# Attention scores on two 64-column halves of TensorE's array

## The chip, the cores and the metric

One core of a Trainium2 chip runs the whole program. The metric is device time in microseconds (us), lower is better. Most executions of one kernel agree within 0.3%. Engines: PE is TensorE's matmul, PEld its weight load, DVE VectorE, ACT ScalarE, POOL GpSimd.

## The reference, cut to what matters

```python
# x [128 graphs, 64 tokens, 768], adj [128, 64, 64] of 0 and 1; all fp32
h = relu(layernorm(x))
for l in range(2):
    m_left, m_right = h @ W_left[l].T, h @ W_right[l].T
    u_left  = einsum('bih,bjh->bij', h, m_left)  / sqrt(768)
    u_right = einsum('bih,bjh->bij', h, m_right) / sqrt(768)
    u = u_left * (upper triangle of adj and diagonal) + u_right * (lower triangle of adj)
    e = exp(u) * adj
    attention = e / (e.sum(axis=2) + 1e-10)
    h = relu(layer_norm(attention @ (h @ W_lin[l].T + b_lin[l])))
out = x + h
```

The scores of a graph ("batch" below) are a 64x64 matrix for left and one for right.

## The kernel before

A unit is 512 tokens: Q = 4 pairs of batches (PAIR = 2, S = 64 tokens, P = 128). There are 16 units, and each layer has two passes over them: pass one makes m_left and m_right (`project`), the scores and the attention, and pass two makes h @ W_lin (`linear`), attention times that, and the layer norm. The projections use Strassen's scheme, which is why they come as seven groups X, Y, Z, V, X, Z, V of six matmul instructions each. Instructions are issued in the order of the program; `queue` and `pump` mix small steps in between. An evacuation is the instruction of VectorE or ScalarE that takes a finished result of TensorE out of its result memory (PSUM).

The scores before, once with left and once with right:

```python
def scores(u, k, kind):
    ht, m = HT[1, l, u], M[kind]                 # both [128 features, 6 chunks, 512 tokens]
    p = ps_aux.tile([P, Q, P], F32, name="aux")
    for q in range(Q):
        t = slice(q * P, (q + 1) * P)            # a pair of batches: 128 tokens
        for c in range(C):
            nc.tensor.matmul(p[:, q, :], m[:, c, t], ht[:, c, t],      # stationary, moving
                             start=(c == 0), stop=(c == C - 1))
    ...
    for h in range(PAIR):
        r = slice(h * S, (h + 1) * S)
        nc.vector.tensor_tensor(um[r, k], p[r, :, r], wm[r, :, k, :], op=ALU.mult)
    # then, after the second kind: add, exp, times adj,
    #   a matmul with the block matrix bsum for the sums over j, + eps, reciprocal, product, store
```

`p[r, :, r]` shows that two 64x64 blocks of each 128x128 result are used and two are thrown away. The attention is stored as 64 columns per row, and pass two copies it into zeroed block-diagonal matrices (`expand`, on POOL).

## Time and profile before

| | before |
|---|---|
| median of the first 3 runs | 3460.22 us (3458.72 to 3462.4) |
| PE busy | 3258.6 us, 94% of the span |
| score matmuls, busy time of PE | 353.4 us, 3072 records |
| DVE, POOL, ACT busy | 39%, 26%, 16% |

The lines behind this, and how they are read, are in the prediction.

### The profile page before, as it was taken

How to read it: one execution, taken by the hardware profiler on the slowest of the kernel's cores; microseconds unless marked ns; L12 is line 12 of the kernel's file. 1: busy time of each engine (PE TensorE's matmuls, PEld its weight loads, DVE VectorE, ACT ScalarE, POOL GpSimd, SP SyncE). 2: the span in 40 equal slices, each digit the busy share in tenths (PEclk: the TensorE clock that was granted, in tenths of full speed). 3: DMA queues.
4: the chain of work that ended last, by engine and by line, in shares of the span. 5: the costliest groups of instructions: out<-in, count | busy, mean ns of one | idle time of the engine just before them, and what ended most of it. 6: DMA issues, size and time to landing. Idle time of an engine off the chain costs nothing.

```text
span 3456.8 us, 37506 instructions
## 1 busy us (share of the span) xinstructions
PE 3258.6 (94%) x15168; PEld 2574.7 (74%) x15168; DVE 1347.1 (39%) x2938; ACT 537.1 (16%) x1137; POOL 887.6 (26%) x576
## 2 busy tenths in 40 slices
PE   5999999999999879999989999999999979988987
PEld 4898989898989545555568988989989965544544
DVE  4334333433342324444422322232232226666665
ACT  1111111111111123333310000000000001111111
POOL 3000110011010243223222110010010015766675
PEclk9999999999999989999999999999999989999999
DMA  5111121111110222232221100100010012333332
GB/s 173 48 42 46 42 78 42 46 58 62 46 42 20 96 98 98 76 114 77 76 80 51 45 25 24 42 28 24 30 40 24 23 66 100 130 127 124 139 131 102
DMA packets 77484, 236.25 MB, mean 68 GB/s; under 512 B 7936, under 2 KB 42240, under 8 KB 67072
## 3 DMA queue, kind: packets, MB, share of 16 engines
q1 hardware_dynamic: 77312, 233.86, 18.6%
q8 instruction: 119, 1.95, 0.2%
q14 instruction: 53, 0.43, 0.0%
HBM read 154.15 MB, written 79.69 MB: 68 GB/s over the span
## 4 chain that ended last, share of the span: by engine, by line
PE 82%; POOL 9%; DVE 5%; DMA 2%; ACT 1%; issue 1%; SPq 1%; POOLq 0%; ACTq 0%; DVEq 0%
PE V L235 14%; PE Z L235 14%; PE X L235 14%; PE aux L265 10%; PE Y L235 7%; PE X L455 6%; PE aux L374 5%; POOL z L403 4%; PE Y L455 4%; PE V L455 3%; POOL z L402 3%; PE Z L455 2%; DVE xr L405 2%; PE aux L204 1%; PE aux L421 1%; DVE u L463 1%
## 5 line engine op out<-in xcount | busy, mean ns | idle before, releaser
L120 POOL TENSOR_TENSOR ts<-ht 128x768 f32<-128x768 f32 x64 | 115.7, 1808 | 1592.8 <-DMA ht<-h 781.7
L265 PEld LDWEIGHTS aux<-ht,n 128*128 128x128 f32 x3072 | 352.0, 192 | 2.6
L265 PE MATMUL aux<-ht,n 128*128 128x128 f32 x3072 | 353.4, 275 | 0.0
L455 PE MATMUL X<-w_n_A,ht 128*128 128x384 f32 x768 | 280.5, 503 | 65.5 <-DVE n L472 36.4
L455 PE MATMUL V<-w_n_A,ts 128*128 128x384 f32 x768 | 271.6, 490 | 23.6 <-DVE n L470 23.6
L235 PE MATMUL X<-ht,w_l_A 128*128 128x256 f32 x1152 | 281.7, 381 | 12.3 <-DMA ht<-h 12.3
L235 PE MATMUL X<-ht,w_r_A 128*128 128x256 f32 x1152 | 280.1, 379 | 0.0
L235 PE MATMUL V<-ts,w_r_A 128*128 128x256 f32 x1152 | 280.0, 379 | 0.0
L235 PE MATMUL V<-ts,w_l_A 128*128 128x256 f32 x1152 | 280.0, 379 | 0.0
L455 PEld LDWEIGHTS X<-w_n_A,ht 128*128 128x128 f32 x768 | 144.3, 195 | 172.9 <-DVE n L472 54.9
L235 PEld LDWEIGHTS X<-ht,w_l_A 128*128 128x128 f32 x1152 | 217.4, 191 | 41.1 <-DMA ht<-h 12.7
L235 PEld LDWEIGHTS V<-ts,w_l_A 128*128 128x128 f32 x1152 | 218.8, 190 | 29.7
L235 PEld LDWEIGHTS V<-ts,w_r_A 128*128 128x128 f32 x1152 | 216.8, 190 | 28.3
L455 PEld LDWEIGHTS V<-w_n_A,ts 128*128 128x128 f32 x768 | 141.2, 190 | 128.0 <-issue 22.2
L235 PEld LDWEIGHTS X<-ht,w_r_A 128*128 128x128 f32 x1152 | 215.3, 190 | 27.3
L252 DVE TENSOR_TENSOR n<-Z,u 128x256 f32<-128x256 f32 x192 | 81.5, 425 | 364.6 <-PE Z L235 364.6
L240 ACT COPY s<-X 128x256 f32<-128x256 f32 x192 | 71.4, 372 | 974.9 <-PE X L235 974.9
L243 DVE TENSOR_TENSOR u<-Y,s 128x256 f32<-128x256 f32 x192 | 81.6, 425 | 360.6 <-PE Y L235 357.5
L465 POOL TENSOR_TENSOR u2b<-u,b 128x384 f32<-128x384 f32 x64 | 63.7, 995 | 551.3 <-DVE rs L393 551.2
L250 ACT COPY n<-X 128x256 f32<-128x256 f32 x192 | 71.4, 372 | 778.1 <-PE X L235 778.1
L405 DVE SCALAR_TENSOR_TENSOR xr<-z,xr 128x768 f32<-128x768 f32 x64 | 135.8, 2123 | 130.9 <-POOL z L403 130.9
L272 DVE TENSOR_TENSOR um<-aux,wm 64x256 f32<-64x256 f32 x128 | 54.0, 422 | 325.3 <-PE aux L265 324.5
(100 smaller groups left out, 4798.7 us busy)
## 6 DMA issues: line engine op xcount, KB each, us to landing
ht<-h SPq DMA_DIRECT2D x48, 1536.0 KB, 7.5
x<-in_x_dram SPq DMA_DIRECT2D x64, 384.0 KB, 7.2
h<-ht SPq DMA_DIRECT2D x16, 1536.0 KB, 6.2
h<-n SPq DMA_DIRECT2D x16, 1536.0 KB, 6.1
xr<-in_x_dram SPq DMA_DIRECT2D x64, 384.0 KB, 3.7
out_dram<-xr SPq DMA_DIRECT2D x64, 384.0 KB, 2.5
adj<-in_adj_dram SPq DMA_DIRECT2D x32, 256.0 KB, 3.3
w_l_A<-in_w_left_dram SPq DMA_DIRECT2D x8, 576.0 KB, 10.1
```

What stands on the lines that cost most here:

```text
L120: queue.append(lambda: nc.gpsimd.tensor_sub(b["T1"], b["B12"], b["B11"]))
L235: nc.tensor.matmul(p, w[a][:, c, g * P:(g + 1) * P], b[t][:, c, :], start=(new and c == 0), stop=(c == CH - 1), skip_group_check=True)
L240: nc.scalar.copy(s1, p)
L243: nc.vector.tensor_add(u2, p, s1)
L250: nc.scalar.copy(m[:, g, :TH], p)
L252: nc.vector.tensor_add(m[:, g, TH:], p, u2)
L265: nc.tensor.matmul(p[:, q, :], m[:, c, t], ht[:, c, t], start=(c == 0), stop=(c == C - 1))
L374: nc.tensor.matmul(p[:, :HH], BD[u % 2][:, q, :], hl[:, q, n * HH:(n + 1) * HH], start=True, stop=True)
L402: nc.gpsimd.tensor_mul(z, z, rows["a"])
L403: nc.gpsimd.tensor_add(z, z, rows["b"])
L405: nc.vector.scalar_tensor_tensor(xr, z, 0.0, xr, op0=ALU.max, op1=ALU.add)
L455: nc.tensor.matmul(p, b[t][:, c, r * P:(r + 1) * P], w[a][:, c, :], start=(new and c == 0), stop=(c == CH - 1), skip_group_check=True)
```

## The change

The score matrix is turned: tokens i are rows, so that 64 tokens of one batch are the stationary operand, placed in the left or the right half of the array's columns, and m_left and m_right of that batch lie side by side as 128 moving columns. The sums over j then run along a row, which VectorE can do, and bsum goes. The attention must be transposed for pass two, which TensorE does in pass one, and it is stored as a whole block-diagonal matrix, so the copies of pass two go. Cut to its core:

```diff
-    M[kind] = big.tile([P, C, T], F32, name="n")
+    M[u] = [big.tile([P, CH, T // S, 2, S], F32, name="n") for _ in range(2)]   # left, right side by side
...
-            for q in range(Q):
-                t = slice(q * P, (q + 1) * P)
-                for c in range(C):
-                    nc.tensor.matmul(p[:, q, :], m[:, c, t], ht[:, c, t], ...)
+            for q in range(Q):
+                for c in range(C):
+                    for h in range(PAIR):
+                        b = q * PAIR + h
+                        nc.tensor.matmul(p[h * S:(h + 1) * S, q, :], ht[:, c, b * S:(b + 1) * S],
+                                         m[c // CH][:, c % CH, b].rearrange("p k j -> p (k j)"), ...)
...
-                    nc.tensor.matmul(ps, bsum, v, ...)          # sums over j, then 128x256 reciprocal
+                    nc.vector.reduce_sum(s, v, axis=X)          # [128, 4], reciprocal of that
+                    # v * s into the diagonal blocks of bd, then
+                    for q in range(Q):
+                        nc.tensor.transpose(pt[:, q, :], bd[:, q, :], ident)
...
-    nc.gpsimd.tensor_copy(BD[u % 2][k, :, k], AT[u][k])          # pass two
```

Both kinds are now done in one burst per unit, placed between the second and third matmul group of the next unit.

More of the change, by code (lines that the diff above doesn't have):

```diff
@@ L131 @@
     H1 = [dram.tile([P, C, T], F32, name=f"h1_{u}") for u in range(NB)]
-    ATT = [[dram.tile([P, Q, S], F32, name=f"att{l}_{u}") for u in range(NB)] for l in range(L)]
+    ATT = [[dram.tile([P, Q, P], F32, name=f"att{l}_{u}") for u in range(NB)] for l in range(L)]
     ident = const.tile([P, P], F32, name="ident")
@@ L138 @@
     nc.gpsimd.memset(eps_in, EPS_IN)
-    bsum = const.tile([P, P], F32, name="bsum")
-    nc.gpsimd.memset(bsum, 0.0)
     diff = const.tile([P, S], I32, name="diff")
@@ L146 @@
         r = slice(h * S, (h + 1) * S)
-        nc.gpsimd.memset(bsum[r, r], 1.0)
         nc.gpsimd.iota(diff[r], pattern=[[-1, S]], base=0, channel_multiplier=1)
-    nc.vector.tensor_scalar(tri[:, 0, :], diff, 0.0, None, op0=ALU.is_ge)
-    nc.vector.tensor_scalar(tri[:, 1, :], diff, 0.0, None, op0=ALU.is_lt)
+    nc.vector.tensor_scalar(tri[:, 0, :], diff, 0.0, None, op0=ALU.is_le)
+    nc.vector.tensor_scalar(tri[:, 1, :], diff, 0.0, None, op0=ALU.is_gt)
     BD = []
@@ L183, in masks @@
                 WM[u] = sp.tile([P, Q, 2, S], F32, name="wm")
-                t = tri.rearrange("p k s -> p (k s)").unsqueeze(1).to_broadcast([P, Q, 2 * S])
-                nc.gpsimd.tensor_tensor(WM[u].rearrange("p q k s -> p q (k s)"),
-                                        ADJ[u].rearrange("p q k s -> p q (k s)"), t, op=ALU.mult)
+                for k in range(2):
+                    t = tri[:, k].unsqueeze(1).to_broadcast([P, Q, S])
+                    nc.gpsimd.tensor_tensor(WM[u][:, :, k], ADJ[u][:, :, 1 - k], t, op=ALU.mult)
             def prepare(u):
@@ L221, in pass_one, with project @@
             M = {}
-            def project(u, kind, g):
-                b, w = tokens_of((1, l, u)), W[l, kind]
-                if g == 0:
-                    M[kind] = big.tile([P, C, T], F32, name="n")
-                m = M[kind]
+            def project(u, k, g, between=None):
+                b, w = tokens_of((1, l, u)), W[l, "lr"[k]]
                 bank = {}
@@ L237, in project @@
                                          skip_group_check=True)
+                    if i == 2 and k == 0 and g == 0:
+                        M[u] = [big.tile([P, CH, T // S, 2, S], F32, name="n") for _ in range(2)]
+                    if i >= 3:
+                        half, first = ((1, 4), (0, 0), (0, 4), (1, 0))[i - 3]
+                        to = M[u][half][:, g, first:first + 4, k, :]
+                        pb = p.rearrange("p (b s) -> p b s", s=S)
                     if i == 0:
@@ L246, in project @@
                         nc.vector.tensor_add(u4, p, u2)
-                    elif i == 3:
-                        nc.vector.tensor_add(m[:, CH + g, TH:], p, u4)
                     elif i == 4:
-                        nc.scalar.copy(m[:, g, :TH], p)
-                    elif i == 5:
-                        nc.vector.tensor_add(m[:, g, TH:], p, u2)
-                    else:
-                        nc.vector.tensor_add(m[:, CH + g, :TH], p, u2)
+                        nc.scalar.copy(to, pb)
+                    else:
+                        nc.vector.tensor_add(to, pb, (u4 if i == 3 else u2).rearrange("p (b s) -> p b s", s=S))
@@ L255, in project, with scores @@
+                    if i == 1 and between:
+                        between()
                     pump(1)
-            UM = {}
-            def scores(u, k, kind):
-                ht, m = HT[1, l, u], M[kind]
-                p = ps_aux.tile([P, Q, P], F32, name="aux")
+            def scores(u):
+                ht, m = HT[1, l, u], M[u]
+                p = ps_aux.tile([P, Q, 2 * S], F32, name="aux")
                 for q in range(Q):
-                    t = slice(q * P, (q + 1) * P)
                     for c in range(C):
-                        nc.tensor.matmul(p[:, q, :], m[:, c, t], ht[:, c, t],
-                                         start=(c == 0), stop=(c == C - 1))
-                if k == 0:
-                    UM[u] = sp.tile([P, 2, Q, S], F32, name="um")
-                um, wm, adj = UM[u], WM[u], ADJ[u]
-                for h in range(PAIR):
-                    r = slice(h * S, (h + 1) * S)
-                    nc.vector.tensor_tensor(um[r, k], p[r, :, r], wm[r, :, k, :], op=ALU.mult)
-                if k == 0:
-                    return
+                        for h in range(PAIR):
+                            b = q * PAIR + h
+                            nc.tensor.matmul(p[h * S:(h + 1) * S, q, :], ht[:, c, b * S:(b + 1) * S],
+                                             m[c // CH][:, c % CH, b].rearrange("p k j -> p (k j)"),
+                                             start=(c == 0), stop=(c == C - 1))
+                wm, adj = WM[u], ADJ[u]
@@ L276, in chain @@
                 def chain():
+                    um = sp.tile([P, Q, 2, S], F32, name="um", bufs=1)
+                    nc.vector.tensor_tensor(um.rearrange("p q k j -> p (q k j)"), p.rearrange("p q m -> p (q m)"),
+                                            wm.rearrange("p q k j -> p (q k j)"), op=ALU.mult)
+                    yield
                     v = sp.tile([P, Q, S], F32, name="v", bufs=1)
-                    nc.vector.tensor_add(v, um[:, 0], um[:, 1])
+                    nc.vector.tensor_add(v, um[:, :, 0], um[:, :, 1])
@@ L281, in chain @@
                     yield
-                    nc.vector.tensor_mul(v, v, adj[:, :, 0, :])
+                    nc.vector.tensor_mul(v, v, adj[:, :, 1, :])
+                    s = stat.tile([P, Q], F32, name="s", bufs=2)
+                    nc.vector.reduce_sum(s, v, axis=mybir.AxisListType.X)
                     yield
-                    p2 = ps_aux.tile([P, Q, P], F32, name="aux")
-                    ps = p2.rearrange("p q i -> p (q i)")[:, :Q * S]
-                    nc.tensor.matmul(ps, bsum, v.rearrange("p q i -> p (q i)"), start=True, stop=True)
+                    nc.vector.tensor_scalar_add(s, s, EPS_ATT)
+                    nc.vector.reciprocal(s, s)
+                    bd = BD[u % 2]
+                    for h in range(PAIR):
+                        r = slice(h * S, (h + 1) * S)
+                        nc.vector.tensor_tensor(bd[r, :, r], v[r], s[r].unsqueeze(2).to_broadcast([S, Q, S]),
+                                                op=ALU.mult)
                     yield
-                    s = sp.tile([P, Q, S], F32, name="s", bufs=1)
-                    nc.vector.tensor_scalar_add(s.rearrange("p q i -> p (q i)"), ps, EPS_ATT)
-                    nc.vector.reciprocal(s, s)
                     yield
-                    a = sp.tile([P, Q, S], F32, name="a", bufs=1)
-                    nc.vector.tensor_mul(a, v, s)
-                    nc.sync.dma_start(ATT[l][u], a)
+                    pt = ps_aux.tile([P, Q, P], F32, name="aux")
+                    for q in range(Q):
+                        nc.tensor.transpose(pt[:, q, :], bd[:, q, :], ident)
+                    at = sp.tile([P, Q, P], F32, name="at", bufs=1)
+                    nc.scalar.copy(at, pt)
+                    nc.sync.dma_start(ATT[l][u], at)
                 it = chain()
-                for _ in range(6):
+                for _ in range(7):
                     queue.append(lambda: next(it, None))
@@ L308, in pass_one @@
                 for g in range(CH):
-                    project(u, "l", g)
+                    project(u, 0, g, (lambda: scores(u - 1)) if u and g == 0 else None)
                     if g == 0:
-                        if u:
-                            scores(u - 1, 1, "r")
-                            if u + 1 < NB:
-                                load(u + 1)
+                        if u and u + 1 < NB:
+                            load(u + 1)
                         if u + 1 < NB:
@@ L319, in pass_one @@
                 for g in range(CH):
-                    project(u, "r", g)
-                    if g == 0:
-                        scores(u, 0, "l")
+                    project(u, 1, g)
                 flush()
-            scores(NB - 1, 1, "r")
+            scores(NB - 1)
             flush()
@@ L356, in load @@
                     load_h(2, l, u)
-                AT[u] = sp.tile([P, Q, S], F32, name="at")
+                AT[u] = sp.tile([P, Q, P], F32, name="at", bufs=3)
                 nc.sync.dma_start(AT[u], ATT[l][u])
-            def expand(u):
-                for h in range(PAIR):
-                    k = slice(h * S, (h + 1) * S)
-                    nc.gpsimd.tensor_copy(BD[u % 2][k, :, k], AT[u][k])
             def prepare(u):
                 sums_t((2, l, u))
-                queue.append(lambda: expand(u))
             def context(u, q):
@@ L373, in context @@
                     p = ps_aux.tile([P, T], F32, name="aux")
-                    nc.tensor.matmul(p[:, :HH], BD[u % 2][:, q, :], hl[:, q, n * HH:(n + 1) * HH],
+                    nc.tensor.matmul(p[:, :HH], AT[u][:, q, :], hl[:, q, n * HH:(n + 1) * HH],
                                      start=True, stop=True)
```

## The prediction

> **What bounds the kernel now**
>
> I read the table of busy time by stretch first, because the four passes (scores of layer one, contexts of layer one, then both for layer two) may have different limits. Its columns: stretch in us, length, busy us and instruction count of PE, PEld, DVE, ACT and POOL, then granted clock, DMA share, GB/s.
>
> ```profile
> 100.00:1100.00 1000.00, 1000.00 (x5471) 899.11 (x5470) 354.89 (x813) 163.53 (x319) 117.33 (x70) 1.00 0.14 49
> 1140.00:1700.00 560.00, 518.34 (x1792) 311.86 (x1793) 233.20 (x601) 163.02 (x336) 168.19 (x128) 0.97 0.26 97
> 1770.00:2820.00 1050.00, 1048.30 (x5584) 942.44 (x5585) 292.48 (x617) 77.54 (x208) 146.72 (x84) 1.00 0.09 31
> 2850.00:3450.00 600.00, 530.99 (x1580) 297.03 (x1579) 380.98 (x733) 91.77 (x192) 402.46 (x248) 0.99 0.33 122
> ```
>
> In the first and third stretch, the two score passes, TensorE has practically no gap, and no other engine is busy for 40% of the time. What leaves TensorE's stream there comes off the end; work on other engines is free as long as it keeps up. In the second and fourth TensorE is idle for 7 and 12%.
>
> Second, the groups of instructions:
>
> ```profile
> L265 PE MATMUL aux<-ht,n 128*128 128x128 f32 x3072 | 353.4, 275 | 0.0
> L235 PE MATMUL V<-ts,w_r_A 128*128 128x256 f32 x1152 | 280.0, 379 | 0.0
> ```
>
> L265 is the scores. The program has 1536 such products (16 units x 2 layers x 2 kinds x 4 pairs of batches x 6 chunks), so 3072 records mean that one fp32 product is two weight loads and two matmuls. The means (275, 379 ns) are latencies of overlapping instructions, not costs. The cost is the distance from one start to the next, so third the timeline of TensorE (start us, length us):
>
> ```profile
> 184.71 5.52 PE L265 MATMUL aux<-ht,n 128*128 128x128 f32 x48
> 190.07 1.46 PE L235 MATMUL X<-ht,w_l_A 128*128 128x256 f32 x6
> 191.37 1.46 PE L235 MATMUL Y<-ts,w_l_S 128*128 128x256 f32 x6
> ...
> 195.25 0.59 PE L286 MATMUL aux<-v,bsum 128*128 128x256 f32 x2
> 195.69 1.46 PE L235 MATMUL X<-ht,w_l_A 128*128 128x256 f32 x6
> ...
> 212.52 0.60 PE L204 MATMUL aux<-ident,x 128*128 128x128 f32 x4
> 212.96 1.46 PE L235 MATMUL V<-ts,w_r_A 128*128 128x256 f32 x6
> ```
>
> Starts subtracted: a score burst takes 190.07 - 184.71 = 5.36 us, 112 ns for each of its 48 matmuls of 128 columns. Six projection matmuls of 256 columns take 1.30 us, 216 ns each; four transposes 0.44 us, 109 ns each; the two matmuls with bsum 0.44 us. One unit of pass one in layer one is then 252 x 0.216 = 54.4 us of projections, 2 x 5.36 = 10.72 us of scores, 0.44 of bsum, 24 x 0.109 = 2.6 of transposes: 68.2 us, which is also the distance of every second burst in the chain of waits (116.70, 151.88, 184.88 us). So scores are 10.72 x 32 = 343 us, 10% of the kernel. The columns say where the waste is: two batches share the 128 stationary columns, and of each 128x128 result only the two diagonal 64x64 blocks are used.
>
> Fourth, the last pass, because the change takes a copy from POOL there:
>
> ```profile
> 3182.21 0.84 POOL L363 COPY bd<-at 64x256 f32<-64x256 f32 x2
> 3185.05 0.99 POOL L465 TENSOR_TENSOR u2b<-u,b 128x384 f32<-128x384 f32 x1 [2.00 <-DVE rs L393]
> ```
>
> After the copy POOL idles 2 us for VectorE, so the copy holds nobody up.
>
> **What the Trainium skill says**
>
> "TensorEngine Tiling (Array Packing)", section Tiling Modes: the array can be two tiles of 128 rows x 64 columns that load weights and multiply in parallel, and changing the mode drains the engine. The change uses this: the built program gives its 1536 score products tiles of 128x64, half of them at column 0 and half at 64. The kernel before uses the full array alone, so its trace can neither confirm nor deny it.
>
> "TensorE: Matmul & The Clock Gate", Part 3: matmuls start and end strictly in program order; three column tiles of 32 columns, moving 512, measured 2.38 times the speed of one. No fp32 figure is given, and fp32 with its two loads and two matmuls per product is what matters here.
>
> Same page, section LDWEIGHTS: loading takes (stationary columns)/1.2 ns, so an estimated 107 ns for 128 columns and 53 ns for 64. The trace agrees for 128: in a score burst each load starts within 0.01 us of the preceding matmul's start, and 107 ns plus a few ns on either side is the 112 ns found.
>
> **The change part by part**
>
> 1. Scores. Removed per unit: two bursts of 48, 10.72 us. Added: one burst of 96 (64 stationary columns, 128 moving, both kinds at once). The instruction count does not change. All of the gain must come from two half-array matmuls running at once. If they do, the pair costs what one matmul costs now: 96 x 112 / 2 = 5.4 us. I allow a little more, since two loads of an estimated 53 ns plus the few ns each just fill the time of one matmul: 96 x 57 ns = 5.5 us.
>
> 2. Mode changes, two per burst. The full-array matmuls must drain before the first half load and the reverse. A projection matmul's latency of 379 ns is 163 ns more than its pace of 216, and a load that is hidden today is then exposed. I estimate 0.25 us per change, 0.5 us per burst.
>
> 3. bsum (0.44 us) leaves, four transposes of the attention (4 x 0.109 = 0.44 us) come: nothing on TensorE.
>
> 4. VectorE per unit. Removed: four 64x256 products (4 x 0.42), the sum's add (0.43), the 128x256 reciprocal (1.75), the product (0.86): 4.7 us. Added: one 128x512 product from PSUM (about 0.7, extrapolated from 425 ns at 256 and 558 ns at 384), the row sum (about 0.4), two tiny ones (0.15 and 0.17), two 64x256 products (0.84): 2.3 us. ACT gets a copy of 128x512, about 0.6 us as in the turning of x (597 ns). All off the path, as both have over half their time free.
>
> 5. New waits. The order of instructions on TensorE has the burst of unit u-1 after the first two groups (X, Y) of unit u, 2.6 us after the last projection, so VectorE's last result (0.42 us) is long there. The new rows go to buffers that the burst has just read: the first such write follows the V group, two groups after the burst. The four transposes stand seven groups (9 us) after the burst, while the chain to the diagonal blocks is some 5 us of work interleaved on VectorE and ACT. No new wait is expected.
>
> 6. Pass two loses the copies (64 x 0.39 us of POOL, idle afterwards) and reads 256 KB instead of 128 KB per unit at a DMA share of 0.3: zero.
>
> Sum: 5.5 + 0.5 = 6.0 us in place of 10.72, 4.7 x 32 = 151 us less: 3460 - 151 = 3309 us.
>
> **Rivals**
>
> A. The halves overlap in part. The two passes of one product are neighbours in the stream and use the same half. If the load for the other half cannot pass a matmul that still waits for its own half, a cycle of four matmuls is: start, wait 107 ns for the half, load 53 ns with some ns around it, wait for the other half to end, load again: 2 x (109 + 58) = 334 ns, 83 ns each, 8.0 us per burst. With the drains 8.5, saving 2.2 x 32 = 71 us: 3389. For it: loads in the trace start just after the matmul before them, as an in-order engine would do it. Against it: the same is seen if the load waits only for its weight buffer, and the section quoted reports that loads are pulled ahead.
>
> B. No overlap for fp32. Then 96 x 109 ns = 10.5 us (load hidden behind the matmul) plus 0.5 for drains: 11.0, 0.3 x 32 = 9 us more, 3469. For it: nothing in the trace shows two matmuls at once. Against: the skill's measurement.
>
> C. Slower. If in the half mode a load cannot hide under a matmul, each costs 53 + 109 = 162 ns, 15.6 us per burst: 3460 + 156 = 3616. Against: loads hide in every group of the present trace.
>
> D. The gain is made but a wait in front of TensorE returns it. Against: part 5; it would need some microseconds in each unit, and the slack is 2.6 us or more everywhere I looked.
>
> **Range and chances**
>
> Full overlap with 55%, partial (A) 20%, none (B) 18%, slower (C, D) 7%. Full overlap covers 3285 (no drain at all) to 3330. A straddles the limit of 2%, which is 3391 us. So faster 0.68, within 2% 0.26, slower 0.06. I predict 3315, a little above the sum because every departure I can think of is upward; the range from 3285 to 3460 holds full and partial overlap and the edge of none.
>
> **What would show each step**
>
> Full overlap: score bursts in the timeline of 5.2 to 6 us for 96 matmuls, 55 to 60 ns apart, weight loads with half their 190 ns or a bit more; units of pass one near 63.5 us instead of 68.2; busy PE near 100% in the two score passes, with the saving split evenly between them. A shows 80 to 90 ns, B 109 ns. Drains show as gaps of 0.2 to 0.3 us at both edges of a burst. A wait of TensorE for VectorE or ACT at the transposes or the first V group would refute part 5. Pass two's unit should stay at some 37 us in the second layer. The prediction is wrong if the time is above 3391, most likely by A or B, or if it is below 3285, which would need a gain outside the scores that I have not seen.

## The result, and the profile after

| | before | after |
|---|---|---|
| median of 4 runs | 3461.22 us | 3297.38 us |
| lowest, highest | 3458.72, 3462.4 | 3296.74, 3302.72 |
| PE busy | 3258.6 us | 3095.9 us |

The ratio is 0.9531 (95% interval 0.9514 to 0.9547). A ratio here is the mean time of one kernel's fast runs over that of the other's of the same rounds, so not quite the ratio of the medians quoted.

First the stretches (columns as in the prediction). They start and end earlier now, so the two outer columns are not comparable, but the shares are:

```profile
100.00:1000.00 900.00, 900.00 (x5416) 795.88 (x5415) 316.56 (x785) 169.35 (x326) 119.36 (x84) 1.00 0.16 56
1060.00:1620.00 560.00, 521.85 (x1805) 313.84 (x1805) 235.58 (x612) 165.12 (x341) 158.78 (x100) 0.97 0.27 101
1690.00:2660.00 970.00, 966.91 (x5610) 853.39 (x5612) 253.15 (x600) 87.52 (x222) 144.14 (x99) 1.00 0.10 34
2690.00:3290.00 600.00, 531.05 (x1575) 296.85 (x1574) 380.17 (x732) 91.88 (x192) 392.46 (x219) 0.98 0.34 125
```

TensorE is still full in the first score pass, and nearly so in the second (3.1 us idle of 970, before 1.7 of 1050). The last stretch is as it was (530.99 us busy of 600 before). The waits in front of TensorE show one that is new, before the four transposes of the attention, where bsum had waited before (engine, output, line, what it waited for: us in total, times, longest). First the kernel before, then the changed one, and one of the long cases in the timeline; a bracket there gives TensorE's idle time before a group and what it waited for:

```profile
PE aux L286 <- DVE v L282: 4.8, 2, 2.4
```

```profile
PE aux L293 <- DVE bd L287: 10.8, 6, 4.0
1054.71 0.66 PE L293 MATMUL aux<-ident,bd 128*128 128x128 f32 x4 [3.99 <-DVE bd L287]
```

Two of the six stand at the end of the score passes, where no projections are left to cover VectorE's steps. The other four (0.62 to 0.76 us) are in the second layer. This takes 6 us off the gain.

Then the score group of the changed kernel:

```profile
L263 PE MATMUL aux<-n,ht 128*64 128x128 f32 x3072 | 174.7, 274 | 0.0
```

The count is the same 3072, and the length of one is the same (274 ns, 275 before). Only the busy time has halved, from 353.4 to 174.7 us. Instructions of unchanged number and length that cover half the time are lying on top of each other. A slice of 10 ns in the middle of a burst shows how many are under way, before and after (the average is 3072 x 275 ns / 353.4 us = 2.4 before and 3072 x 274 / 174.7 = 4.8 after):

```profile
186.83 0.39 PE L265 MATMUL aux<-ht,n 128*128 128x128 f32 x2
```

```profile
232.82 0.39 PE L263 MATMUL aux<-n,ht 128*64 128x128 f32 x4
```

Last, the timeline of TensorE around one burst of the changed kernel (start us, length us):

```profile
229.42 1.46 PE L229 MATMUL Y<-ts,w_l_S 128*128 128x256 f32 x6
230.81 5.46 PE L263 MATMUL aux<-n,ht 128*64 128x128 f32 x96
236.20 1.56 PE L229 MATMUL Z<-ts,w_l_S 128*128 128x256 f32 x6
237.60 1.46 PE L229 MATMUL V<-ts,w_l_A 128*128 128x256 f32 x6
```

Start to start, the 96 matmuls take 5.39 us. The group before takes 1.39 us and the one after 1.40 us where such groups take 1.30, so the edges cost 0.09 + 0.10 us more. That is 5.58 us in place of 10.72, and 32 x 5.14 = 164 us. The medians differ by 163.8 us and the two profiled runs by 160.9, so the score bursts are the gain to within the few us of the new wait and of smaller shifts. In the chain of waits, bursts of the first layer now follow each other at 63.06 us:

```profile
167.82 5.39 PE aux L263 x96
230.88 5.39 PE aux L263 x96
```

### The profile page after: what moved, and what is told of

It is laid out like the page before. It is cut to its first block, busy times and chain, and to the rows that moved or that the text cites. A ratio compares the mean times of both kernels' runs of the same rounds, so it can differ in the third digit from the quotient of the medians.

```text
span 3295.9 us, 37473 instructions
## 1 busy us (share of the span) xinstructions
PE 3095.9 (94%) x15232; PEld 2396.5 (73%) x15232; DVE 1269.5 (39%) x2906; ACT 557.6 (17%) x1169; POOL 867.5 (26%) x541
## 4 chain that ended last, share of the span: by engine, by line
PE 81%; POOL 9%; DVE 5%; DMA 2%; ACT 1%; issue 1%; SPq 1%; POOLq 0%; ACTq 0%; DVEq 0%
PE Z L229 15%; PE V L229 15%; PE X L229 15%; PE Y L229 8%; PE X L447 6%; PE aux L263 5%; PE aux L366 5%; POOL z L395 4%; PE Y L447 4%; PE V L447 4%; POOL z L394 3%; PE Z L447 2%; DVE xr L397 2%; PE aux L413 1%; PE aux L200 1%; DVE u L455 1%
## 5 line engine op out<-in xcount | busy, mean ns | idle before, releaser
L447 PE MATMUL X<-w_n_A,ht 128*128 128x384 f32 x768 | 282.2, 505 | 61.0 <-DVE n L464 36.4
L250 DVE TENSOR_TENSOR n<-V,u 128x256 f32<-128x256 f32 x384 | 162.2, 422 | 284.5 <-PE V L229 283.5
L366 PE MATMUL aux<-n,at 128*128 128x384 f32 x512 | 176.1, 486 | 0.7 <-DVE n L464 0.5
L263 PE MATMUL aux<-n,ht 128*64 128x128 f32 x3072 | 174.7, 274 | 0.0
```

What stands on the lines that cost most here:

```text
L250: nc.vector.tensor_add(to, pb, (u4 if i == 3 else u2).rearrange("p (b s) -> p b s", s=S))
L263: nc.tensor.matmul(p[h * S:(h + 1) * S, q, :], ht[:, c, b * S:(b + 1) * S], m[c // CH][:, c % CH, b].rearrange("p k j -> p (k j)"), start= ...
L366: nc.tensor.matmul(p[:, :HH], AT[u][:, q, :], hl[:, q, n * HH:(n + 1) * HH], start=True, stop=True)
L447: nc.tensor.matmul(p, b[t][:, c, r * P:(r + 1) * P], w[a][:, c, :], start=(new and c == 0), stop=(c == CH - 1), skip_group_check=True)
```

## The experiments

The theory was that the gain is two matmuls at a time, one in each half. Rivals: smaller weight loads, or the other parts of the change. All kernels below gave correct results.

**Order of the products: 24 left, then 24 right.** The same instructions, only neighbours now share a half.

```diff
-                for q in range(Q):
-                    for c in range(C):
-                        for h in range(PAIR):
+                for h in range(PAIR):
+                    for q in range(Q):
+                        for c in range(C):
```

> The changed kernel, but all 24 products of the left half of the array come first and then all 24 of the right half. Instructions, loads, columns and sizes are the same; only neighbours in the stream now use the same half. Theory 1 (the gain is two matmuls running side by side, started in program order): only one pair at the seam can overlap, so a burst of 96 takes about 95 x 109 ns = 10.4 us instead of 5.4, and the kernel takes 3297 + 32 x 5.0 = 3457 us, the time of the kernel before. Theory 2 (the gain comes from the smaller weight load or from the other parts of the change): 3297 us. Theory 3 (each half has a deep queue of its own, so the order does not matter): the instruction window would have to hold 48 pairs; 3297 us if it does.

Measured: 3457.08 us, ratio to the kernel before 0.999 (0.9975 to 1.0004). The whole gain is gone although every load is still of 64 columns. A slice of 10 ns inside a burst:

```profile
242.75 0.49 PE L263 MATMUL aux<-n,ht 128*64 128x128 f32 x3
```

```profile
240.70 10.24 PE aux L263 x96
```

The second line is the burst in the chain of waits: 10.24 us for 96 is one every 107 ns, where the changed kernel takes one every 56 (5.39 us for 96). So halves alone give nothing; the gain is the side by side, and it depends on the order of the stream. The number is that of theory 1, but its "started in program order" is not shown by it: the next runs show a reach past some three waiting matmuls, which at the one seam of this run is worth only an estimated 4 x 0.109 = 0.4 us.

**Blocks of six products and of two.** How far may neighbours share a half before the overlap is lost?

```diff
+ e2_blocks6:  for q:  for h:  for c in range(6):  matmul
+ e2_blocks2:  for q:  for c0 in (0, 2, 4):  for h:  for c in (c0, c0 + 1):  matmul
```

> The six products of one batch stand together (12 matmuls on one half, then 12 on the other). Matmuls started strictly in program order: 11 of 12 starts wait for their own half, so 96 x 109 x 11/12 = 9.6 us per burst, 3297 + 32 x 4.2 = 3431 us. If the engine can start work of the other half past waiting matmuls (12 pairs ahead): 5.4 us, 3297 us.

> Two products of one batch stand together (4 matmuls on one half, then 4 on the other). Strictly in program order: 3 of 4 starts wait for their own half, 96 x 109 x 3/4 = 7.9 us per burst, 3297 + 32 x 2.5 = 3377 us. With a window that looks a few pairs ahead: 5.4 us, 3297 us.

Measured: 3382.1 us with six (ratio 0.9776) and 3301.39 us with two (0.9539). Both readings that I had put down for six were wrong: the strict order wanted 3431, free choice 3297. The slices show what happens. In blocks of six, 0.08, 0.61 and 1.21 us into a burst:

```profile
236.69 0.32 PE L263 MATMUL aux<-n,ht 128*64 128x128 f32 x1
```

```profile
237.07 0.49 PE L263 MATMUL aux<-n,ht 128*64 128x128 f32 x3
```

```profile
237.62 0.54 PE L263 MATMUL aux<-n,ht 128*64 128x128 f32 x5
```

The first half runs alone (one, then three under way), and then both run (five). In the trace's start times the second half starts with the ninth matmul of the first half's twelve: three are still waiting for their half, and the engine reaches past them. So the last four matmuls of a block overlap with the first four of the next, and a pair of blocks repeats every 1.86 us instead of 2.6. With blocks of two products, which are four matmuls, the reach is just enough. The start of such a burst:

```profile
230.57 0.34 PE L264 MATMUL aux<-n,ht 128*64 128x128 f32 x2
```

Two have started within 14 ns of each other, though one half takes its matmuls 109 ns apart and the first two products of the program, four matmuls, belong to one half. The second to start must belong to the third product, while the second product has not started. So a matmul waiting for its half does not hold back the other half, as long as no more than about three wait. The trace does not name the half of a record; this follows from the spacing.

**Everything of the change except the halves.** Both batches stationary in all 128 columns, 256 columns moving, half of each result unused (so VectorE's product with the mask comes in four pieces and not in one).

```diff
-                            nc.tensor.matmul(p[h * S:(h + 1) * S, q, :], ht[:, c, b * S:(b + 1) * S],
-                                             m[c // CH][:, c % CH, b], ...)
+                        nc.tensor.matmul(p[q // 2][:, q % 2], ht[:, c, q * P:(q + 1) * P],
+                                         m[c // CH][:, c % CH, q * PAIR:(q + 1) * PAIR], ...)
```

> Everything of the change except the two halves: both batches of a pair are stationary in all 128 columns and 256 columns move, so half of every result is unused as before. Theory 1: 48 matmuls of 256 columns x 216 ns = 10.4 us per burst, no mode change, so 3297 + 32 x (10.4 - 5.6) = 3450 us: the rest of the change (the row sum in place of the bsum product, the transposed attention, no copies in pass two, one burst instead of two) is worth some 10 us at most[...]. Theory 2 (the rest of the change carries part of the gain): clearly below 3440 us.

Measured: 3448.35 us, ratio 0.9963 (0.9947 to 0.998). Its burst:

```profile
240.64 10.36 PE aux L261 x48
```

That is 32 x (10.72 - 10.36) = 12 us of the 13. Row sums, transposes and the missing copies are worth nothing by themselves.

**Four bursts instead of one.** It measures what the edges of a burst cost.

```diff
-                    if i == 1 and between:
-                        between()                       # all four pairs of batches
+                        if between and (i == 1 or (i == 0 and c == CH - 1)):
+                            part(u - 1, 0 if i == 0 else c + 1)      # one pair
```

> The changed kernel with its score burst cut into four, one pair of batches each, with full-array projection matmuls between them; three more bursts, so six more mode changes per unit, nothing else. In the trace of the changed kernel the first half matmul starts 309 ns after the last full one (216 without a change) and the second full matmul 320 ns after the first (216): 0.2 us per burst. Theory 1 (this is what a mode change costs): 3297 + 32 x 3 x 0.2 = 3316 us. The prediction's estimate of 0.5 us per burst: 3345 us. Free mode changes: 3297 us.

Measured: 3330.68 us, ratio 0.9626. That is 33 us above the changed kernel where I expected 19. The timeline says why:

```profile
167.03 1.53 PE L267 MATMUL aux<-n,ht 128*64 128x128 f32 x24
168.49 0.70 PE L229 MATMUL Y<-ts,w_l_S 128*128 128x256 f32 x2
169.12 1.53 PE L267 MATMUL aux<-n,ht 128*64 128x128 f32 x24
```

A burst and two full matmuls take 2.09 us. Twelve pairs at 0.109 us and two matmuls at 0.216 us would be 1.74, so a burst costs 0.35 us at its edges. My 0.2 had counted only the gaps outside the burst and not the 0.16 us inside the 5.39 us (48 x 0.109 = 5.23), where the first pair is exposed to its loads and the last is waited for. With 0.35: 3297.4 + 32 x 3 x 0.35 = 3331 us, as measured. One burst for both kinds is therefore worth about 11 us against two.

**The kernel before with halves, and nothing else.** Stationary 64 rows of one batch and kind, moving the 64 tokens of that batch.

```diff
-                        nc.tensor.matmul(p[:, q, :], m[:, c, t], ht[:, c, t], ...)
+                        for h in range(PAIR):
+                            r = slice(h * S, (h + 1) * S)
+                            t = slice(q * P + h * S, q * P + (h + 1) * S)
+                            nc.tensor.matmul(p[r, q, r], m[:, c, t], ht[:, c, t], ...)
```

> The kernel before with only its score products changed: the 64 rows of one batch and kind stationary in one half, the same batch's 64 tokens moving, so 96 products of 64x64 results per unit instead of 48, in two bursts. Bank, masks, bsum product and everything after are as before. If a half takes a 64-column matmul in [...](56 to 58 ns, worked out from 109 and 216 ns at 128 and 256) and the loads keep up: 48 x 58 = 2.8 us per burst, with 0.2 us of mode change twice per unit 6.0 us in place of 10.72, 3461 - 151 = 3310 us, so the rows and the joint left and right are not needed for the gain. If such small matmuls are held up by loads or by issuing (109 ns each as for 128 columns): 10.5 + 0.4 us per unit, 3467 us.

Measured: 3318.45 us, ratio 0.9589: 87% of the gain (143 of 164 us) for four lines. The chain of waits has its bursts, two per unit, each as

```profile
147.40 2.95 PE aux L267 x96
```

which is 2 x (2.95 + 0.2) = 6.3 us per unit against 5.58. Some 0.35 us of the difference is the second burst's edges. The rest is the pace: in the trace's start times a half takes a matmul of 64 moving columns every 58 ns, and each load begins 2 ns after its half's previous matmul has started, and the next matmul starts 56 ns after the load. The paces of 109 and 216 ns at 128 and 256 moving columns give an estimate of 55.5 ns for 64, so the load, and not the moving columns, seems to set the pace of 58 here; no run separates the two. Left and right side by side avoid this.

**A try for more: quarters in pass two.** The attention matrix is block-diagonal, so half of the stationary operand is zeros.

```diff
-                    nc.tensor.matmul(p[:, :HH], AT[u][:, q, :], hl[:, q, n * HH:(n + 1) * HH], ...)
+                    for s in range(PAIR):                # batch of the pair: half of the rows
+                        k = slice(s * S, (s + 1) * S)
+                        for t in range(2):               # pair: half of the columns
+                            q = 2 * t + r
+                            nc.tensor.matmul(cx[s][n][t * S:(t + 1) * S], AT[u][k, q, k],
+                                             hl[k, q, n * HH:(n + 1) * HH], ...)
```

> A try for a faster kernel: the changed kernel, and in pass two the products of attention with hl on four 64x64 quarters of the array (a batch's 64 tokens in one half of the rows, two pairs of batches in the two halves of the columns), instead of block-diagonal 128x128 attention whose other half is zeros. Rows of a tile then hold the same batch of two pairs, and x and the output move in blocks of 64 rows. TensorE's time for them: 512 matmuls x 322 ns = 165 us now, half if four quarters run at once, 82 us less, minus about 64 x 0.2 us of mode changes, 70 us at most. In the second layer's pass two TensorE waits for VectorE already, so part of it comes back as waiting there: I expect 3240 to 3270 us. If quarters do not run at once, 16 matmuls per step x 322 ns: 3297 + 165 us and more.

Measured: 3292.73 us, ratio 0.9513. The quarters do run at once (in the trace's start times four matmuls start within 20 ns of each other, and fours follow at some 0.3 us), and nearly nothing came of it. The timeline of the last pass, first of the changed kernel, then with quarters:

```profile
3111.43 2.74 PE L366 MATMUL aux<-n,at 128*128 128x384 f32 x8
3114.01 2.10 PE L447 MATMUL Y<-w_n_S,ts 128*128 128x384 f32 x6
...
3124.54 2.20 PE L447 MATMUL V<-w_n_A,ts 128*128 128x384 f32 x6 [0.69 <-DVE n L462]
3128.78 2.20 PE L447 MATMUL X<-w_n_A,ht 128*128 128x384 f32 x6 [2.04 <-DVE n L464]
```

```profile
3119.42 1.52 PE L369 MATMUL aux<-n,at 64*64 64x384 f32 x16
3120.87 2.20 PE L455 MATMUL Y<-w_n_S,ts 128*128 128x384 f32 x6
...
3132.18 2.17 PE L455 MATMUL V<-w_n_A,ts 128*128 128x384 f32 x6 [1.37 <-DVE n L470]
3134.74 2.20 PE L455 MATMUL X<-w_n_A,ht 128*128 128x384 f32 x6 [0.39 <-DVE n L472]
```

The products fell from 2.58 to 1.45 us. But the bracket of the next V group, the wait for VectorE's evacuation n, grew from 0.69 or 0.78 us to 1.26 to 1.37: TensorE arrives earlier and waits longer. (The brackets of X alternate between 0.39 and some 2.04 us in both kernels; their sum, 36.4 us, is the same.) VectorE's timeline of the same stretch has the reason, a step that stands before that evacuation and waits for POOL (2.55 us long, then the evacuation):

```profile
3129.01 2.55 DVE L403 SCALAR_TENSOR_TENSOR xr<-z,xr 128x768 f32<-128x768 f32 x1 [3.09 <-POOL z L401]
3131.49 0.55 DVE L470 TENSOR_TENSOR n<-V,u 128x384 f32<-128x384 f32 x1
```

The sums of start-to-start times over the last pass say how much each took: the products lost 34 us, the wait before V grew by 18, and the groups next to the products (the last X before them and Y after them, where the array changes its mode) grew by 13. In the first layer's pass two the products lost 35 us, the turning of the result (transposes that wait for ACT) grew by 19 and the edges by 6. So waiting took back about half in each pass, and the changes of mode a good part of the rest.

**The same two kernels with that step issued later.** Six empty queue steps put VectorE's last step behind the next two evacuations; in the first layer two empty steps delay the turning of the result, before which TensorE waited for ACT.

```diff
                 for i in range(len(a)):
+                    if i == 4 and last:
+                        queue.extend([lambda: None] * 6)
                     queue.append(a[i])
                     queue.append(b[i])
-                return [lambda: next(it, None)] * (5 if last else 4)
+                return [lambda: next(it, None)] * 5
```

> The changed kernel with the order in pass two moved only: in the last layer the final step of each row group (VectorE's maximum and residual, which waits for GpSimd) is issued two to three product groups later, behind VectorE's next two evacuations; in the first layer the turning of the result is issued two queue steps later. In the trace of the changed kernel TensorE waits some 60 us in the last pass for evacuations that stand behind that step. If the order is the cause, most of it goes: 3297 - 50 = 3247 us, and the last pass's unit of 37.2 us comes to 34 us. If GpSimd's rate is the cause (25 us of 37 busy), nothing moves: 3297 us.

> The same move of order on the kernel with quarters in pass two. The quarters take 1.1 us per group from TensorE (1.45 us in place of 2.58 us), 64 groups, 72 us, of which only 5 us reached the end because the wait for VectorE and ACT grew. If that wait is one of order, both gains add: 3297 - 50 - 60 = about 3190 us. If pass two is held by GpSimd and VectorE, it gives the same as the later order alone, about 3250 us.

Measured: 3214.3 us (ratio 0.9288) for the changed kernel with the later order, 3179.55 us (0.9187) with quarters as well. The order was the cause: in the first of the two the V and X groups of the last pass follow each other without a bracket.

```profile
3037.37 2.10 PE L449 MATMUL V<-w_n_A,ts 128*128 128x384 f32 x6
3039.30 2.10 PE L449 MATMUL X<-w_n_A,ht 128*128 128x384 f32 x6
3041.24 2.10 PE L449 MATMUL Z<-w_n_S,ht 128*128 128x384 f32 x6
3043.17 2.10 PE L449 MATMUL V<-w_n_A,ts 128*128 128x384 f32 x6
3045.11 2.10 PE L449 MATMUL X<-w_n_A,ht 128*128 128x384 f32 x6
```

It gave 83 us where I expected 50: I had counted the 59 us of waits named on the V and X groups of the last pass, while TensorE was idle for 69 of 600 us in that stretch, and I had counted nothing for the move in the first layer. From the first to the last projection matmul, the last pass fell from 598 to 527 us, and the first layer's pass two from 599 to 585. Quarters then add 35 us, where they gave 5 before, but short of the 60 I expected; the timeline with quarters still has a wait of 1.06 us for VectorE in the middle of the products of some units, where evacuations now crowd (17.9 us in 16 such waits, against 8.7 with the later order alone). The shortfall is in the last pass: quarters took 27 us from the first layer's pass two and only 11 from the last. Whether that wait is all of the missing 25 us was not tested. The kernel with both is the fastest found, 8.1% under the kernel before.

## Why the prediction was right

It said 3315 us with a sum of 3309; the time was 3297.38. By its own steps:

1. Scores, 5.5 us per burst: right in kind, 0.1 us too high. The halves run side by side (e1 takes it away by order alone), 96 matmuls in 5.39 us including 0.16 us of its edges. The pace of a pair is 109 ns and not the 114 I allowed, because each half hides its own loads (a load starts 2 ns after its half's matmul, as in the kernel before). A load of 64 columns lasts 137 ns in the trace, against 192 for 128, so more than the "half their 190 ns or a bit more" of the prediction.
2. Mode changes, 0.5 us per burst: too high. 0.2 us lies outside the burst, 0.35 us in all, confirmed by e4. Together with step 1: 5.58 instead of 6.0 us, 32 x 0.42 = 13 us. The sum lies 12 us above the result: these 13 us, less the 6 us of step 5, and some 4 us of smaller shifts that were not traced.
3. bsum against transposes: e3 shows the rest of the change at 13 us, 12 of them from the score burst itself (48 matmuls of 256 columns take 10.36 us, 96 of 128 columns 10.72), so nothing for this exchange, as said.
4. VectorE and ACT: off the path. VectorE's busy time fell from 1347.1 to 1269.5 us, 2.4 us for each of the 32, as worked out (4.7 - 2.3), and nothing came of it.
5. No new wait: nearly right. TensorE is at 900.00 of 900 us in the first score pass, but the kernel waits for VectorE at the transposes, which the prediction had named as what would refute this part: 10.8 us in all, where bsum had cost 4.8. The prediction had put the chain to the diagonal blocks at 5 us against 9 us of cover. At the end of a pass there is no cover, and the wait is 3.99 us where it was 2.41. In four units of the second layer VectorE's second product into the diagonal blocks takes 1.94 to 2.08 us in place of 0.42, each time beside a sum of 1.8 to 1.9 us on POOL; nine other products that overlap with POOL are not slower, so the cause stays open. The two score passes also did not save evenly: from its first projection matmul to the first of pass two, the one of the first layer is 83 us shorter and that of the second 77.
6. Pass two: right; its last stretch has 531.05 us of TensorE in 600 us, before 530.99.

Rival A (partial overlap) did not happen in the changed kernel, but not for the reason I gave. It described a strict order in which a load cannot pass a waiting matmul. Blocks of six products show that matmuls themselves are passed, up to about three waiting ones. The chosen order, two fp32 matmuls per half in turn, lies within that reach; e2_blocks6 is a partial overlap, by another mechanism. Rival B's number (3469) is near what e1 gave without overlap (3457; its burst was 10.24 and not 10.5 us, since even there the seam overlaps). Rival C left no trace; rival D is the 6 us of step 5. The 6 us that I added to the sum "because every departure is upward" went the wrong way: the two large departures were downward, and the closeness of 3309 to the result owes something to step 5 going the other way.

## What to carry to other kernels

Where two small independent products each use half of the array's columns, put them on two halves and alternate between them in the stream every few instructions: the gain is the alternation, and the same halves in long blocks gave none of it. Keep enough moving columns per matmul to hide its load (128 for a 64-column load here), and gather such products in one burst, because entering and leaving cost 0.35 us. Before taking work from TensorE in another stretch, look at the brackets behind it: where it already waits for another engine's evacuation, the order on that engine has to be mended first, or the gain comes back as waiting.

## What the Trainium skill lacked or had wrong

- "TensorE: Matmul & The Clock Gate", Part 3, says that matmuls start strictly in program order. The block runs contradict it for two column halves in fp32: a matmul of the free half starts before waiting ones of the other half that stand ahead of it, past about three of them. With blocks of four matmuls the burst is 5.44 us, of twelve 7.96 us, of 48 10.24 us. The part also has no fp32 case for column tiles: here two 64-column halves run at 2.0 times one, a pair every 109 ns where each half alone takes one every 109 ns.
- The same page, section LDWEIGHTS: the estimate of 53 ns for a load of 64 columns fits, as a half with 64 moving columns runs at 58 ns per matmul. No run shows alone that the load sets this pace.
- "TensorEngine Tiling (Array Packing)", Tiling Modes, says that a change of mode drains the engine but not what it costs: 0.35 us here for entering and leaving a burst together. It has no fp32 figure for 64x64 quarters either: 16 matmuls of 384 moving columns took 1.45 us, against 2.58 us for the 8 full-array ones that they replace, with edges of 0.2 to 0.4 us per group besides.
